# First transfers, scales and skip weights of a four-layer gated kernel in another order

## The chip, the cores and the metric

The kernel runs on one core of a Trainium2 chip. The core has five engines that work side by side and wait for each other through semaphores: TensorE (PE in the profile; PEld is its weight load), VectorE (DVE), ScalarE (ACT), GpSimd (POOL) and SyncE (SP), which here only issues transfers (DMAs). Every engine takes its own instructions in order. The metric is the time of one execution on the device in microseconds, as the median of several runs. A profile is one execution with every instruction recorded.

## The reference

The input `x` is 16 batches of 128 rows by 256 columns in float32, with a context of the same shape. Four layers follow each other; each adds a gated attention-like step and a gated feed-forward step to `x`:

```python
x = x + jnp.tanh(g_xattn[0]) * _L0_xattn_ref(ctx_2048, ctx_2048, _layernorm(x, axis=-1), L0_xattn_ssm_kernel, L0_xattn_D, 8)
x = x + jnp.tanh(g_ffn[0]) * _L0_ffn_ref(_layernorm(x, axis=-1), ...)
...
x = x + jnp.tanh(g_ffn[3]) * _L3_ffn_ref(_layernorm(x, axis=-1), L3_ffn_A, L3_ffn_B, L3_ffn_Wr, L3_ffn_br)
```

The change is in the first step. It forms the products of the context with itself within each head of 8 rows, convolves them along the 256 columns with the head's kernel, adds the products times a skip weight `D`, and weighs the result with the normalised `x`:

```python
kv = jnp.einsum('bhil,bhjl->bijhl', k_, v_)
...
y = jnp.fft.irfft(kv_f * kernel_f, n=fft_size)[..., :L]
out = y + kv * D[None, None, None, :, None]
out = jnp.einsum('bijhl,bhil->bjhl', out, q_)
```

The other steps are a mixture of experts, grouped attention, a quantised feed-forward layer, a retention, a second mixture of experts, a channel attention and a routed low-rank layer.

## The kernel before

**The start** (`stage_l0x`, line 461) is the first step. Its order of work on each engine is written out by hand (line 465). `x` comes in four groups of four batches, `xg[0]` to `xg[3]`; groups 0 and 1 are asked for on ACT's queue (lines 389 and 390), 2 and 3 on SP's (lines 590 and 591). The context comes transposed, in two halves of eight batches, by indirect gathers on POOL (`gathered`, line 363), two issues per half. The convolution is a matmul with a Toeplitz matrix per head: four transfers on SP (line 588) bring four heads each into `T[0]` to `T[3]`, a 128 by 256 block per head. The skip weight of a head is added on DVE to the antidiagonal of its block's first half, in place (line 608); `skips` holds the weights (line 393).

For each group `stats` (line 472) takes mean and variance on DVE, `scaled` (line 478) makes scale and offset with three operations on POOL, `normal` (line 488) applies them (on ACT; for group 1 on DVE, line 493), and `turn` (line 497) transposes the result on PE and copies it with ACT. Groups 2 and 3 get their sums from ACT (`scaled_by_act`) during the loop.

The loop (line 625) runs over 32 half heads: 16 heads for each of two halves of the batches. For each, `products` (line 520) multiplies context rows on POOL, in two operations (lines 527 and 528); `convolved` (line 531) runs 12 matmuls on PE; `weighed` (line 547) multiplies the result by the normalised `x` on DVE, in two operations (lines 551 and 552), and for some half heads POOL adds two halves of it (line 555); `summed` (line 557) reduces it on DVE. Iteration `n` weighs `n`, convolves `n + 2`, makes the products of `n + 4` and sums `n - 2`. Six buffers hold products, three hold convolutions. Before the loop come the first products and convolutions, and a loop over the 16 heads (lines 606 to 613) that adds all skip weights, with the normalisation of group 1 after the second and the reduction `some` of the mask after the tenth.

**The expert layer** (`stage_moe0`) follows from about 100 to 260 us, with its order by hand too. SP loads its weights during the start.

**The planned stage** (`stage_rest`, line 1183) is everything else, to the end. A list of operations goes to a planner (`Plan`, line 100), which picks at each step, per engine, among operations that are ready the one with the least target time plus biases: for a change of ACT's table, for a change of PE's mode, and for PE's idle time. The target of an operation is an entry of one of the `T_` tables plus an entry of `BASES` (lines 41 to 85); the biases are line 40:

```python
BIASES = 0.27, 158.38, 2.24, 0.00, 3.82
```

They are the window, the two biases for table and mode, the one for idle time, and a hold for wide results. Targets decide the order alone.

Of the kernel before, what the change touches and what calls it, by code (L numbers as in the profile page):

```python
# [11 lines left out]
F32 = mybir.dt.float32  # L12
# [3 lines left out]
ALU = mybir.AluOpType  # L16
AX = mybir.AxisListType
PSUM = bass.MemoryType.PSUM

P = 128  # L20
B = 16
# [15 lines left out]
NSH = 9  # L37
PAIR = 1
N_K1, N_K2, N_K4, N_R2, N_X = 10, 9, 5, 4, 7
BIASES = 0.27, 158.38, 2.24, 0.00, 3.82  # L40
T_ONCE = [
    -43.5, 143.5, 65.9, 105.9, -39.2, 199.6, -61.2, 86, 110.2, 143.6, 119.7, 115.6, 86.5, 65.9, 97.7, 4.3, -130.6,
    -31.9, -83.7, -176.3, -222, -116.8,
]
T_SHARED = [
    -108.2, -94.6, -22, -76.2, -45.3, -33.5, -4.1, -135.1, -8.9, 127.9, -47.6,
]
T_GROUPED = [
    -98.3, 41.7, 87, -96, -142.1, 41.2, 20, 103.7, -31.8, 38.5, 65.2, -33.5, 105.3, 116.7, -11.8, 15.6, 5.6, 10.4, 48,
    93.6, 22.1, -23.5, -1.1, 24.6, 24, 33.6, 88.5, 39, 44.3, 74.3, 49.7, 82.9, 62.6, 35, 15.8, 53.7, -88.1,  # L50
]
T_QUANTISED = [
    74.6, 108.2, 143.8, 35.5, -20.4, 108.8, 93.2, 70.8, 54.8, 0.9, 56.9, 75.7, 44.1, 78.4, 22.4, 76.5, 76.9, 78.3,
    68.4, 112.1, 95.9, 101.6, 168.9, 71.1, 70.5, 160.4, 125.7, 66.7, 86.5, 81.7, 88.9, 3.9,
]
T_RETENTION = [
    60.8, 125.2, 70.9, 96.4, 85.4, 184.2, 100.8, 158.9, 94.8, 114.2, 85.3, 76.2,
]
T_EXPERTS = [
    -18.4, 71.7, 93.4, 160.1, 16, 135.7, 102.6, 68.2, 141.5, 103.8, 168.9, 114.9, 137.7, 94.1, 66.8, 91.5, 63.4,  # L60
    117.2, 130.4, 135.6, 102.3, 81.9, 82.6, 136.4, 76.6, 117, 149.9, 147.8, 163.1, 49.5, 105.5, 66.3, 127.3, 116,
    63.5, 79.9, 129.9, 129.4, 243.9, 222, 155.6, 193.1, 140.4, 110.2, 84.4, 144, 133.2, 120.2, 112.1, 120.8, 152.2,
    151.4, 143.8, 119.1, 73.1, 148.2, 140.3, 171.3, 134.9, 139.5, 186.8, 147.2, 118.4, 105.7, 150.5, 149.6, 115.6,
    112.6, 101.4, 68.6,
]
T_CHANNEL = [
    106.3, 121.5, 94.5, 209.2, 127.9, 260.4, 293.5, 134.3, 140.5, 133.7, 128.7, 148.1, 303, 213.1, 146.4, 193, 142.3,
    140.6, 151.8, 126.6, 118, 194.7, 170.1, 152.9, 110.2, 143.9, 136.8, 170.3, 184.7, 172.7, 116.6, 100.5, 102.5,
    180.1, 162.7, 310.9, 187.6, 224.5, 189.8, 179.8, 191.8, 191.2, 236.3, 195.2, 230.7, 339.1, 313.4, 176.2, 162.1,
    179.1, 199.2, 177.8, 189.2, 185.4, 200.9, 265.5, 110.7, 187.9, 292.7, 192.9, 203.6, 214, 206.4, 264.8, 215.4,  # L70
    203.5, 198.3, 209.9, 204.3, 216.5, 310.7, 221.5, 193.6, 203.4, 223.9, 215.2, 227.3, 221.3, 275.4,
]
T_LOW_RANK = [
    397.4, 354.4, 300.9, 203.2, 200.5, 224.6, 225.4, 240.3, 233.7, 228.6, 226.9, 174.6, 163.2, 189.9, 262.2, 248.6,
    174.2, 209.8, 194.7, 253.1, 331.3, 215.7, 312.5, 243.8, 330.4, 253.6, 242.6, 202.8,
]
BASES = [
    -30.9, 31.3, -42.3, -30, -43.2, 35.7, 52.7, -91, -49.1, -4.9, -46.5, -16.6, -11.7, 30.9, -13.9, 41.5, 16.4, 23.3,
    8.9, 71.6, 56.7, 52.3, 67.2, 63, 63.8, 114.1, 95.4, 94.2, 108.9, 108.2, 48.7, 149.2, 150.6, 140.8, 143.9, 147.1,
    152.2, 191.7, 175.1, 210.6, 188.2, 190.8, 189.1, 232, 216.9, 224.2, 232.5, 229.3, 202.4, 271.9, 245.5, 273.5,  # L80
    268.1, 270, 274.8, 315.8, 317.8, 288.7, 312.9, 311.8, 316.5, 359.4, 348.6, 365.3, 355.4, 349.3, 358.2, 398.6,
    377.3, 409.5, 394.9, 392.3, 392.4, 438.6, 432.8, 421.6, 435.1, 433.5, 424.6, 465, 442.4, 462.7, 468.3, 468.4, 492,
    506.8, 485.5, 500.4, 493.9, 497.4, 575.3, 540.8, 525.4, 550.1, 524.4, 529.8, 628.8, 566, 560.1, 545.6, 558, 557.2,
    591,
]


# [257 lines left out]
def kernel(ctx: ExitStack, tc: tile.TileContext, a: dict, out: bass.AP):  # L345
    nc = tc.nc
# [9 lines left out]
    s0 = s0e.enter_context(tc.tile_pool(name="s0", bufs=1, side="right"))  # L356
# [6 lines left out]
    def gathered(u):  # L363
        for c in range(2):
            nc.gpsimd.indirect_dma_start(
                out=ctxT[:, u, c, :],
                out_offset=None,
                in_=a["ctxT"].rearrange("d (u b) s -> (d u) (b s)", u=2),
                in_offset=bass.IndirectOffsetOnAxis(ap=back[:, u, c : c + 1], axis=0),
            )  # L370
# [6 lines left out]
    anti = s0.tile([P, P], F32, name="anti")  # L377
# [8 lines left out]
    def asked(eng, g):  # L386
        eng.dma_start(xg[g], a["x"][g * GB : (g + 1) * GB].rearrange("b p d -> p b d"))

    asked(nc.scalar, 0)
    asked(nc.scalar, 1)  # L390
    T = [s0.tile([P, 4, D], F32, name=f"toep{q}") for q in range(4)]
    skips = s0.tile([P, B], F32, name="skips")
    nc.sync.dma_start(skips, a["L0_xattn_D"].partition_broadcast(P))
# [13 lines left out]

    tg = cst.tile([P, 8], F32, name="tg")
    for i, n in enumerate(("g_xattn", "g_ffn")):
        nc.gpsimd.dma_start(tg[:, 4 * i : 4 * i + 4], a[n].partition_broadcast(P))  # L410

    neghalf = cst.tile([P, GB], F32, name="neghalf")
    nc.gpsimd.memset(neghalf, -0.5)
# [47 lines left out]
    def stage_l0x(xTs, anyk, kba, rowsd, loads, xs, xnp, xns, rss, offs):  # L461

        with tc.tile_pool(name="s0w", bufs=2) as s0w, tc.tile_pool(name="s0t", bufs=2, space=PSUM) as pst, tc.tile_pool(
            name="s0y", bufs=3, space=PSUM
# [4 lines left out]
            mb = s0.tile([B, P], F32, name="mb")  # L469
            mvs, tmp = {}, {}  # L470

            def stats(g, of=range(GB)):
                if of[0] == 0:
                    mvs[g] = s0w.tile([P, GB, 2], F32, name="mv", bufs=4), s0w.tile([P, GB, 6], F32, name="st", bufs=4)
                mv, st = mvs[g]
                statistics([xg[g][:, k, :] for k in of], mv[:, of[0] :], st[:, of[0] :])

            def scaled(g):
                mv, _ = mvs[g]
                ve = s0w.tile([P, GB], F32, name="ve", bufs=4)  # L480
                scale_offset(mv, ve, rss[:, g], offs[:, g])
# [6 lines left out]
            def normal(g):  # L488
                tmp[g] = s0w.tile([P, GB, D], F32, name="xn")
                if g != 1:  # L490
                    return normalised(tmp[g], xg[g], rss[:, g], offs[:, g])
                for k in range(GB):
                    nc.vector.tensor_scalar(
                        tmp[g][:, k, :], xg[g][:, k, :], rss[:, g, k : k + 1], offs[:, g, k : k + 1], ALU.mult, ALU.add
                    )
# [94 lines left out]
            asked(nc.sync, 2)  # L590
            asked(nc.sync, 3)
            loads()
            gathered(1)
            warm = pst.tile([P, 512], F32, name="tp")
            for k in range(24):
                nc.tensor.transpose(warm[:, k % 4 * P : k % 4 * P + P], ident, ident)
            stats(0)
            scaled(0)
            nc.gpsimd.dma_start(rows[1:2, :], a["mask"].rearrange("(o b) s -> o (b s)", o=1))
            nc.gpsimd.dma_start(mb, a["mask"])  # L600
            stats(1)
            normal(0)
            products(0)
            scaled(1)
            turn(0)
            for n in range(B):
                t = T[n // 4][:, n % 4, 0:P]
                nc.vector.scalar_tensor_tensor(t, anti, skips[:, n : n + 1], t, ALU.mult, ALU.add)
                if n == 1:
                    normal(1)  # L610
                if n == 9:
                    some = s0.tile([B, 1], F32, name="some")
                    nc.vector.tensor_reduce(some, mb, AX.X, ALU.max)
            products(1)
            convolved(0)
            turn(1)
            products(2)
            convolved(1)
            products(3)
            scales = {}  # L620
            for g in (2, 3):
# [3 lines left out]
            for n in range(N):  # L625
                if n == N - 4:
                    turned(0)
                if n + 2 < N:
                    convolved(n + 2)
                if n in (18, 20, 22, 24):  # L630
                    back_turn(n - 18)
                weighed(n, n % 5 in (1, 3) or n >= 26)
                if n + 4 < N:
                    products(n + 4)
                if n > 1:
                    summed(n - 2)
                if n in (3, 5):
                    g = 2 + n // 5
                    scales.pop(g)()
                    normalised(tmp[g], xg[g], rss[:, g], offs[:, g])  # L640
                if n in (6, 10):
                    turn(2 + n // 10)
                if n == 9:
                    masks()
                if n in (18, 20, 22, 24):
                    added(n - 18)
                if n in (20, 24):
                    scales[n // 24] = scaled_by_act(n // 24, kept_tile(n // 24))
                if n in (22, 26):
                    scales.pop(n // 26)()  # L650
                    kept(n // 26)
# [1548 lines left out]
```

## Time and profile before

| what | value |
|---|---|
| median of 3 runs | 1080.39 us (1078.98 to 1081.77) |
| profiled execution | 1072.21 us, of it 1070.2 us between first and last instruction (the span) |
| PE, DVE, ACT, POOL busy | 91%, 69%, 57%, 50% of the span |
| granted TensorE clock, mean | 0.973 of full speed |
| start's loop, first weighing | 26.45 us |
| expert layer, about | 100 to 260 us |

A line of a timeline gives an instruction's start in us from the span's start, its duration, its engine, its line in the kernel, the operation, and what it writes and reads; a bracket at the end is the time that the engine stood idle before it and what ended that. Several equal instructions in a row are one line with a count. `toep` are the Toeplitz blocks, `kv` the products, `y` the convolutions, `pr` the weighed results, `xn` a normalised group, `tp` a transposed one, `st` and `mv` the statistics, `rss` and `offs` scale and offset.

### The profile page before, as it was taken

The page shows a single profiled execution, that of the slowest core. Times are in us where ns is not written, and L with a number is a line of the kernel's source. Part 1 is how long each engine was busy: PE and PEld are TensorE (multiplying, and loading weights), DVE is VectorE, ACT ScalarE, POOL GpSimd, SP SyncE. Part 2 cuts the span into 40 slices and gives each one's busy share as a digit, 9 for nine tenths or more (in the row PEclk, how much of TensorE's full clock was granted, in tenths as well). Part 3 has the DMA queues.
Part 4 walks back from the last instruction along what each step waited for, and adds up shares of the span by engine and source line. Part 5 has one row for each costly group of instructions (what it writes and reads, how often), then busy time and mean ns, then how long its engine had stood idle before and what let it go on. Part 6 is the DMA issues. An engine that isn't in the chain of part 4 may idle for free. (4 is left out here: it accounts for less than half of the span.)

```text
span 1070.2 us, 20227 instructions
## 1 busy us (share of the span) xinstructions
PE 978.4 (91%) x7076; PEld 715.2 (67%) x7076; DVE 736.9 (69%) x1763; ACT 612.0 (57%) x1066; POOL 538.3 (50%) x1027
## 2 busy tenths in 40 slices
PE   6998999998987898889999899899999999999987
PEld 5887777776665665756667576676766667567644
DVE  5998655524566587757687787787768778777643
ACT  3416422322255446767675867768777488676752
POOL 7899255421345653544465554755636462744311
PEclk8999999999998888999999999999999999999999
DMA  9712524344920033030321303313130303232220
GB/s 296 157 39 83 184 65 113 99 99 108 334 80 21 30 80 95 17 99 17 105 71 61 106 17 109 101 36 95 32 99 23 99 24 84 86 100 71 56 47 15
DMA packets 75152, 92.39 MB, mean 86 GB/s; under 512 B 10345, under 2 KB 65321, under 8 KB 75049
## 3 DMA queue, kind: packets, MB, share of 16 engines
q1 hardware_dynamic: 67276, 73.55, 24.2%
q0 software_dynamic: 6720, 16.51, 5.6%
q8 instruction: 57, 0.93, 0.4%
q10 hardware_dynamic: 1056, 1.05, 0.3%
q14 instruction: 43, 0.35, 0.1%
HBM read 57.51 MB, written 30.56 MB: 82 GB/s over the span
## 5 line engine op out<-in xcount | busy, mean ns | idle before, releaser
L1849 DVE TENSOR_REDUCE sg<-ps 128x4 f32<-128x1024 f32 x128 | 153.3, 1216 | 38.8 <-PE ps L1837 37.0
L1905 ACT ACTIVATE k<-ps 128x1024 f32<-128x1024 f32 x128 | 127.9, 1029 | 21.4 <-PE ps L1894 19.1
L1702 PE MATMUL ps<-L2w,r 128*128 128x512 f32 x384 | 101.4, 408 | 2.3 <-ACT k L1905 1.3
L1727 POOL TENSOR_TENSOR k<-k,sg 128x352 f32<-128x352 f32 (+4 forms) x112 | 56.2, 524 | 80.0 <-DVE k L1715 63.9
L1702 PEld LDWEIGHTS ps<-L2w,r 128*128 128x128 f32 x384 | 69.5, 189 | 21.5 <-ACT k L1905 3.2
L1327 POOL TENSOR_TENSOR sm<-sm,kconsts 128x1 f32<-128x1 f32 x96 | 19.9, 209 | 126.1 <-DVE sm L1326 119.8
L539 PE MATMUL y<-kv,toep 128*128 128x128 f32 (+1 forms) x384 | 70.0, 341 | 6.4 <-DVE pr L552 3.9
L1349 ACT COPY k<-pa 128x256 f32<-128x256 f32 (+1 forms) x79 | 35.0, 445 | 63.4 <-PE pa L1342 48.6
L539 PEld LDWEIGHTS y<-kv,toep 128*128 128x128 f32 x384 | 61.4, 198 | 14.4 <-issue 3.6
L1837 PE MATMUL ps<-gk,gq 64*128 64x256 f32 x512 | 57.9, 317 | 11.6 <-DMA gq<-dq 5.7
L1894 PE MATMUL ps<-gq,gk 64*128 64x256 f32 x512 | 60.0, 321 | 5.7 <-DVE nc L1454 1.6
L1837 PEld LDWEIGHTS ps<-gk,gq 64*128 64x128 f32 x512 | 38.4, 188 | 36.8 <-issue 16.4
L1342 PE MATMUL pa<-ident,k 128*128 128x128 f32 x268 | 51.0, 291 | 10.1 <-POOL k L1332 3.8
L933 POOL DMA_INDIRECT xb<-xs,who x40 | 39.4, 984 | 41.4 <-PE tb L945 33.2
L1894 PEld LDWEIGHTS ps<-gq,gk 64*128 64x128 f32 x512 | 38.6, 187 | 32.2 <-issue 10.7
L1328 POOL TENSOR_TENSOR sm<-sm,kconsts 128x1 f32<-128x1 f32 x96 | 55.3, 576 | 6.4
L1332 POOL TENSOR_SCALAR k<-x,sm 128x256 f32<-128x256 f32 x96 | 53.8, 561 | 7.5
L1325 DVE BATCH_NORM_STATS2 sm<-x 128x6 f32<-128x256 f32 x96 | 40.5, 422 | 21.1 <-POOL x L1954 11.9
L963 PE MATMUL ub<-L0we,xbT 128*128 x160 | 50.7, 460 | 0.2 <-ACT xbT L947 0.2
L1342 PEld LDWEIGHTS pa<-ident,k 128*128 128x128 f32 x268 | 31.1, 144 | 28.6 <-POOL k L1332 6.5
L1914 PE MATMUL pa<-k,v 128*32 128x256 f32 x768 | 49.1, 383 | 1.1 <-ACT k L1771 0.8
L1712 ACT ACTIVATE k<-ps 128x512 f32<-128x512 f32 x48 | 28.5, 597 | 32.9 <-PE ps L1702 26.7
(442 smaller groups left out, 2541.3 us busy)
## 6 DMA issues: line engine op xcount, KB each, us to landing
gq<-dq SPq DMA_DIRECT2D x64, 192.0 KB
dk<-r SPq DMA_DIRECT2D x32, 256.0 KB
gk<-dk SPq DMA_DIRECT2D x64, 128.0 KB
dq<-r SPq DMA_DIRECT2D x32, 256.0 KB
ys<-ysb SPq DMA_DIRECT2D x20, 256.0 KB
L0we<-in_L_w_dram SPq DMA_DIRECT2D x6, 704.0 KB
L2w<-in_L_w_dram POOLq DMA_DIRECT2D x3, 768.0 KB, 8.8
toep<-in_kpad_dram SPq DMA_DIRECT2D x4, 512.0 KB
```

The costliest lines, as they stand in the source:

```text
L539: nc.tensor.matmul(dst, lhsT=T[n % B // 4][:, n % 4, d : d + P], rhs=kv[k][:, H * mc : H * mc + H], start=(mc == 0 and k == 0), stop=(mc = ...
L963: nc.tensor.matmul(t[:, i, 0 : 2 * I], lhsT=xbT[:, i, c, :], rhs=we[:, bass.ds(regs[s][i] + c * 2 * I, 2 * I)], start=(c == 0), stop=(c == 1),
L1328: op("POOL", 0.53, lambda: G.tensor_tensor(s.t[:, 11:12], s.t[:, 10:11], nhalf, ALU.pow), r=[s], p=[s])
L1332: lambda: G.tensor_scalar(xn.t, x.t, s.t[:, 8:9], s.t[:, 11:12], ALU.add, ALU.mult),
L1342: lambda: [T.transpose(t.t[:, c * P : (c + 1) * P], xn.t[:, c * P : (c + 1) * P], ident) for c in range(n)],
L1702: T.matmul(u.t[:, 512 * k : 512 * k + 512], lhsT=xv()[:, m // 2, m % 2], rhs=wt[:, m // 2, c0 : c0 + 512], start=(m == 0), stop=(m == 3),)
L1727: G.tensor_tensor(v, v, bc(c(12)[:, e : e + k], 2, (hi_ - lo_) // k), ALU.mult)
L1837: T.matmul(mv[:, h, jj, :], lhsT=q.t[r, o + (t0 + n) * P : o + (t0 + n + 1) * P], rhs=k.t[r, o : o + D], start=True, stop=True,)
L1849: lambda m=m, nm=nm, ii=ii, tt=t0 + n: S.tensor_reduce(nm.t[:, 0:16].rearrange("p (t h j) -> p t h j", t=2, h=2)[:, tt, :, 2 * ii : 2 * ii ...
L1894: T.matmul(sv[:, h, jj, :], lhsT=k.t[r, o + (c0 + n) * P : o + (c0 + n + 1) * P], rhs=q.t[r, o : o + D], start=True, stop=True,)
L1905: op("ACT", 1.03, lambda s=s, pt=pt: A.activation(pt.t, s.t, AF.Exp), r=[s], w=[pt], tbl="exp")
L1914: T.matmul(av.t[g_ : g_ + 32, ii * D : (ii + 1) * D], lhsT=vt.t[:, sc, 8 * h + 4 * jh + 2 * ii + jj, :], rhs=pv[:, h, jj, :], start=(sc == 0),
```

## The change

The start is reordered; no operation is added or taken away there. Groups 0 and 1 of `x` and the two gate vectors are asked for on SP's queue. POOL makes the scales of groups 0 and 1 before the first products. The second gather and the two transfers of the mask come behind the third product. Skip weights of heads 0 to 3 are added before the normalisation of group 1 and those of heads 4 to 7 behind it; those of heads 8 to 15 go into the first four iterations of the loop, two in each, and `some` into the fifth. The transpose of group 1 goes ahead of the first convolution on PE. The planned stage gets new target times and biases; its operations stay.

```diff
-BIASES = 0.27, 158.38, 2.24, 0.00, 3.82
+BIASES = 0.27, 154.01, 2.49, 0.00, 3.84
 T_ONCE = [
-    -43.5, 143.5, 65.9, 105.9, -39.2, 199.6, -61.2, 86, 110.2, 143.6, 119.7, 115.6, 86.5, 65.9, 97.7, 4.3, -130.6,
+    -59.8, 128.2, 45.3, 90.8, -64.4, 173.4, -76.7, 71.1, 104.3, 141.6, 130.2, 109.8, 88.5, 89.8, 114.2, 17.6, -141.3,
...
-    asked(nc.scalar, 0)
-    asked(nc.scalar, 1)
+    asked(nc.sync, 0)
+    asked(nc.sync, 1)
...
     for i, n in enumerate(("g_xattn", "g_ffn")):
-        nc.gpsimd.dma_start(tg[:, 4 * i : 4 * i + 4], a[n].partition_broadcast(P))
+        nc.sync.dma_start(tg[:, 4 * i : 4 * i + 4], a[n].partition_broadcast(P))
...
             loads()
-            gathered(1)
             warm = pst.tile([P, 512], F32, name="tp")
             for k in range(24):
                 nc.tensor.transpose(warm[:, k % 4 * P : k % 4 * P + P], ident, ident)
+
+            def with_skip(n):
+                t = T[n // 4][:, n % 4, 0:P]
+                nc.vector.scalar_tensor_tensor(t, anti, skips[:, n : n + 1], t, ALU.mult, ALU.add)
+
             stats(0)
             scaled(0)
+            stats(1)
+            scaled(1)
+            normal(0)
+            products(0)
+            turn(0)
+            for n in range(4):
+                with_skip(n)
+            normal(1)
+            products(1)
+            turn(1)
+            convolved(0)
+            for n in range(4, 8):
+                with_skip(n)
+            products(2)
+            convolved(1)
+            gathered(1)
             nc.gpsimd.dma_start(rows[1:2, :], a["mask"].rearrange("(o b) s -> o (b s)", o=1))
             nc.gpsimd.dma_start(mb, a["mask"])
-            stats(1)
-            normal(0)
-            products(0)
-            scaled(1)
-            turn(0)
-            for n in range(B):
-                t = T[n // 4][:, n % 4, 0:P]
-                nc.vector.scalar_tensor_tensor(t, anti, skips[:, n : n + 1], t, ALU.mult, ALU.add)
-                if n == 1:
-                    normal(1)
-                if n == 9:
-                    some = s0.tile([B, 1], F32, name="some")
-                    nc.vector.tensor_reduce(some, mb, AX.X, ALU.max)
-            products(1)
-            convolved(0)
-            turn(1)
-            products(2)
-            convolved(1)
             products(3)
...
                 weighed(n, n % 5 in (1, 3) or n >= 26)
+                if n < 4:
+                    with_skip(8 + 2 * n)
+                    with_skip(9 + 2 * n)
+                if n == 4:
+                    some = s0.tile([B, 1], F32, name="some")
+                    nc.vector.tensor_reduce(some, mb, AX.X, ALU.max)
                 if n + 4 < N:
```

All the other tables (`T_SHARED` to `T_LOW_RANK` and `BASES`) get new numbers in the same way, most of them within some 20 of the old ones.

## The prediction

> **What bounds the kernel now.** I read the page first, then the windows (busy time by stretch), then the timelines of the first 40 us, engine by engine.
>
> The engine shares, from the page:
> ```profile
> PE 978.4 (91%) x7076; PEld 715.2 (67%) x7076; DVE 736.9 (69%) x1763; ACT 612.0 (57%) x1066; POOL 538.3 (50%) x1027
> ```
> TensorE (PE) is the busiest, but not everywhere. The windows (length, then PE, PEld, DVE, ACT, POOL busy, PE clock, DMA share, GB/s):
> ```profile
> 27.00:60.00 33.00, 31.60 (x184) 28.63 (x185) 30.83 (x44) 12.58 (x34) 30.51 (x38) 0.95 0.65 142
> 60.00:75.00 15.00, 14.83 (x94) 13.57 (x93) 14.45 (x22) 1.42 (x7) 13.58 (x17) 1.00 0.11 33
> 75.00:100.00 25.00, 22.23 (x130) 18.73 (x129) 24.37 (x36) 12.17 (x39) 23.46 (x28) 1.00 0.13 43
> ...
> 340.00:440.00 100.00, 87.88 (x621) 65.07 (x619) 71.37 (x177) 52.17 (x87) 54.58 (x113) 0.87 0.21 57
> ...
> 700.00:850.00 150.00, 142.48 (x1216) 100.67 (x1217) 113.96 (x288) 106.69 (x170) 81.88 (x172) 1.00 0.24 67
> ```
> From 27 to 100 us, the loop over 32 half heads, VectorE (DVE) is busy 69.65 of 73 us, with GpSimd (POOL) close behind (67.55). Work on DVE is the limit there: DVE idle time removed before the loop is a gain, DVE work only moved is not. In the planned stage, from 260 us on, PE is the limit, but at 340 to 440 us it is busy 88% at a clock of 0.87, later 95% at 1.00.
>
> DVE's timeline of the start (start, duration, then what; idle time before it in brackets):
> ```profile
> 14.91 0.88 DVE L608 SCALAR_TENSOR_TENSOR toep<-anti,skips,toep 128x128 f32<-128x128 f32 x2
> 17.00 3.38 DVE L493 TENSOR_SCALAR xn<-x,rss,offs__125 128x256 f32<-128x256 f32 x4 [1.21 <-POOL offs__125 L433]
> 20.31 4.46 DVE L608 SCALAR_TENSOR_TENSOR toep<-anti,skips,toep 128x128 f32<-128x128 f32 x8
> 24.69 0.27 DVE L613 TENSOR_REDUCE some<-mb 16x1 f32<-16x128 f32 x1
> 24.88 1.64 DVE L608 SCALAR_TENSOR_TENSOR toep<-anti,skips,toep 128x128 f32<-128x128 f32 x6
> 26.45 0.67 DVE L551 TENSOR_TENSOR pr<-y,qT 128x512 f32<-128x512 f32 x1
> ```
> DVE waits for x until 7.98, then 1.85 and 1.21 us: 11.04 us idle before the first weighing (26.45). Three of the skip additions singly, and the POOL operations beside the first two:
> ```profile
> 20.31 1.12 DVE L608 SCALAR_TENSOR_TENSOR toep<-anti,skips,toep 128x128 f32<-128x128 f32 x1
> 21.36 0.70 DVE L608 SCALAR_TENSOR_TENSOR toep<-anti,skips,toep 128x128 f32<-128x128 f32 x1
> 24.43 0.34 DVE L608 SCALAR_TENSOR_TENSOR toep<-anti,skips,toep 128x128 f32<-128x128 f32 x1
> ```
> ```profile
> 20.20 1.08 POOL L527 TENSOR_TENSOR kv<-ctxT 128x512 f32<-128x512 f32 x1
> 21.25 0.66 POOL L528 TENSOR_TENSOR kv<-ctxT 128x256 f32<-128x256 f32 x1
> ```
> The reader is to see the lock step: beside a product on POOL the same addition lasts as long as the product, 1.12 or 0.70 us; after 23.57, when POOL stands still, 0.34, a new one each 0.26. The four normalisations of line 493 show the same (3.38 us against 1.38 for four of them at 111 us with POOL idle).
>
> **The change, part by part.** As marker I take the start of the fifth weighing, 33.74 us now: by then all moved additions are done in both kernels.
>
> *Transfers.* Moved on SP ahead of the skip weights, the constants and the four Toeplitz transfers: two x transfers (1.02 us of issue on ACT) and two gate vectors (0.62 and 0.59 on POOL). By 15 us 4.06 MB have moved: 2.05 on the gathers' queue, 1.05 of x, 0.96 on SP's. x lands earliest when 1.05 MB go alone at the 370 GB/s seen from 5 us on, about 6.3 us; latest as now, 7.98 and 12.26. I take 6.3 and 8.5. Everything behind them on SP (Toeplitz, x 2 and 3, weights) is issued some 2 us later. x 2 and 3 now end ACT's wait at 22.71 and feed POOL's scales at 36.29; the expert weights wait until 97: covered, and without cover each us late costs one.
>
> *Gather.* The second gather (two issues, 2.33 us with their gap) and the mask's two DMAs (1.16 us) go behind the third product on POOL. Their readers come late (products of the second half near 53 us; the reduction of the mask, now fifth in the loop). Without the second gather's 1 MB the first lands earlier: the first product, 13.73 now, starts between 12.0 and 13.73; I take 12.5, since half of the 2.05 MB on that queue goes away but x and Toeplitz remain.
>
> *Scales first.* POOL makes both scales (1.6 us each) before the products: mean 8.75, scale 10.3; second 11.2, then 12.9, or 0.4 us after the gather. Three products take 3 x (1.04 + 0.62) = 5.0 us: 12.9 to 17.9.
>
> *Four additions, then four normalisations.* Toeplitz 0 lands in 11.5 to 14 us (first addition 14.91 now); I take 12.6. One addition passes freely, six operations fall in lock step with the six products, the last is free (0.35): the second normalisation ends at 18.2, in place of 20.31. Its transposes end 0.9 us later (20.31 to 21.22 now): 19.1. Additions 4 to 7 cost nothing: they pass under the transposes and the first convolution, at 0.26 while POOL issues DMAs; in lock step they would end at 21.5, still before the weighing below.
>
> *First convolution after the second transpose.* On PE it now took 3.67 us at a granted clock of 0.50 (15.63 to 19.30); two took 4.09 at 1.00, 2.05 each. Bounds 2.05 and 3.67; PE is a little busy before, so I take the middle, 2.9: the first weighing starts at 22.0 less a trifle, 21.9, bounds 20.5 to 22.9, in place of 26.45.
>
> *Eight additions in the loop.* From first to fifth weighing 7.29 us pass now. After the change two additions follow each of four weighings, and the mask's reduction (0.27) precedes the fifth. POOL is in products or pair sums (1.28 us) nearly without pause, so I go through it: of the eight, two come when POOL waits for a weighing (0.26 each), six wait for an operation of 1.04, 0.62 or 1.28, mean 0.83 by the pair above: 0.5 + 5.0 + 0.27 = 5.8, less the 0.51 us that DVE waits for PE before the fifth weighing now. The marker lands at 21.9 + 7.29 + 5.3 = 34.5: 0.75 late. DVE waits another 0.51 us at 38.14, and POOL leads by some 2 us then, so most is absorbed. Start: 0, bounds -4.2 (20.5, all eight at 0.26 and no wait: 29.5) and +4 (22.9, all eight behind a sum of 1.28).
>
> [...]
>
> [...]
>
> *Expert layer, 100 to 260 us.* Same instructions, shifted by the start.
>
> *Planned stage.* 810 us; new target times and slightly other biases: same operations and durations, another order. PE is busy 739.8 of it. Bounds: 290 to 440 us has a PE share of 0.866, 560 to 1000 one of 0.947; if a new order lifts the first to the second, 150 x 0.081 = 12 us go; if it drops another 150 us to the first's share, 12 come. The trace favours neither; I take 0, as the operations are the same.
>
> Sum: 0 + 0. The profiled execution took 1072.21 us (span 1070.2 and 2.0 around it), so 1072.2 again; the median of three runs stands 8.2 above it, so 1080.4 in those terms.
>
> **The rivals.** About 0.3%, 3.2 us, is what a measurement of this kernel can tell from no change.
>
> 1. The planned stage gains: the weak 290 to 440 us fill up. For it: PE at 0.866 there and 0.87 clock, so there is room. Against: nothing in the trace says that new targets use it. Two thirds of 12 us: 1072. Chance 0.24.
> 2. The start gains: the additions find POOL waiting, since it runs out of work behind the weighings (now 5.43 us at 23.57). Price up to -4.2: 1076. Chance 0.14. Against: POOL has two DMAs and a product to catch up.
> 3. Slower, by the additions in the loop alone: each of eight waits behind a pair sum, 8 x (1.28 - 0.26) = 8.2 us over free additions, 3.2 over my sum, with the first weighing late besides. It decides from the point where the first weighing plus 12.6 us exceeds 33.74 + 0.5 + 3.2 = 37.4, that is a first weighing after 24.8 us, or additions that cost over 1.2 us each. About 1085. Chance 0.10.
> 4. The planned stage loses as much as it could gain: 1088. Chance 0.19.
> 5. The transfers don't come sooner, as the sum of bytes sets the time: x at 7.98 and 12.26. Then the second scale is ready at 16.8, the first weighing at about 23, start +1: still no measurable change, and part of my forecast's chance.
>
> **How the numbers follow.** Forecast (start near 0, planned stage within 3 us): 0.33, 1080.4 us. Faster is 1 and 2, 0.38; slower 3 and 4, 0.29; within 0.3% the rest, 0.33. Forecast's own range 1077 to 1084. The whole range adds the start's bounds to three quarters of the planned stage's (9 us), 1069 to 1090; it leaves out 2 in 10 or fewer.
>
> **What would show it.** First statistics near 6.3 us, second directly behind; second scale before the first product; the second normalisation's end near 18.2; first weighing at 20.5 to 22.9; the loop's additions at 0.7 to 1.3 us each, not 0.34; fifth weighing near 34.5; loop's end within 2 us of now. In the windows, 100 to 260 us of the same length; the PE share of 290 to 440 us tells rivals 1 and 4. I am wrong if the first weighing comes before 19 us with free additions, or if the planned stage's length moves by over 3 us: its order is what I could not read from the profile.

## The result, and the profile after

The changed kernel took 1087.76 us (median of 11 runs, 1080.47 to 1091.11), the kernel before 1080.79 us (11 runs): ratio over all runs 1.0053, 95% interval 1.0035 to 1.0071 (the medians alone lie 0.64% apart). It is slower, by more than the 0.3% that I had called no change. Two later comparisons gave 1.0012 (0.9987 to 1.0037) and 1.0033 (1.0005 to 1.0062). The profiled execution took 1086.43 us, with a span of 1084.4 us.

First the engine shares of the changed kernel, from its page:

```profile
PE 974.1 (90%) x7076; PEld 709.7 (65%) x7076; DVE 739.9 (68%) x1763; ACT 611.6 (56%) x1066; POOL 538.3 (50%) x1025
```

The work is the same: 739.9 us on DVE against 736.9, less on PE. No engine is busy for more than 3 us longer, so most of the 14 us by which the span is longer are waiting, not work. The windows of the changed kernel (length, then PE, PEld, DVE, ACT, POOL busy, PE clock, DMA share, GB/s):

```profile
27.00:60.00 33.00, 30.49 (x185) 27.32 (x184) 31.74 (x45) 10.10 (x23) 29.68 (x37) 1.00 0.64 137
60.00:75.00 15.00, 14.44 (x87) 12.57 (x86) 14.52 (x21) 0.91 (x4) 13.83 (x17) 1.00 0.15 46
75.00:100.00 25.00, 22.20 (x131) 19.05 (x130) 24.37 (x36) 12.27 (x40) 22.84 (x29) 1.00 0.13 43
...
340.00:440.00 100.00, 80.17 (x624) 56.05 (x621) 73.05 (x193) 57.85 (x98) 58.73 (x117) 0.97 0.23 61
...
700.00:850.00 150.00, 142.79 (x1164) 100.93 (x1165) 113.59 (x308) 112.58 (x179) 81.83 (x173) 0.99 0.25 74
```

DVE is still the limit from 27 to 100 us: 70.63 of 73 us, 69.65 before. Where it lost is seen in its timeline of the start (below it, the fifth weighing and the loop's last reduction of the kernel before):

```profile
4.88 0.43 DVE L426 BATCH_NORM_STATS2 st<-x 128x6 f32<-128x256 f32 x1 [4.88 <-DMA x<-in_x_dram]
...
13.24 3.20 DVE L599 SCALAR_TENSOR_TENSOR toep<-anti,skips,toep 128x128 f32<-128x128 f32 x4 [3.42 <-DMA toep<-in_kpad_dram]
16.36 1.90 DVE L493 TENSOR_SCALAR xn<-x,rss,offs__125 128x256 f32<-128x256 f32 x4
18.18 2.02 DVE L599 SCALAR_TENSOR_TENSOR toep<-anti,skips,toep 128x128 f32<-128x128 f32 x4
23.59 0.69 DVE L551 TENSOR_TENSOR pr<-y,qT 128x512 f32<-128x512 f32 x1 [3.38 <-PE y L539]
...
24.80 0.61 DVE L599 SCALAR_TENSOR_TENSOR toep<-anti,skips,toep 128x128 f32<-128x128 f32 x2
...
26.82 1.63 DVE L599 SCALAR_TENSOR_TENSOR toep<-anti,skips,toep 128x128 f32<-128x128 f32 x2
...
29.57 1.54 DVE L599 SCALAR_TENSOR_TENSOR toep<-anti,skips,toep 128x128 f32<-128x128 f32 x2
...
33.55 1.62 DVE L599 SCALAR_TENSOR_TENSOR toep<-anti,skips,toep 128x128 f32<-128x128 f32 x2
...
35.88 0.69 DVE L551 TENSOR_TENSOR pr<-y,qT 128x512 f32<-128x512 f32 x1
...
102.00 0.69 DVE L558 TENSOR_REDUCE xT<-pr 128x128 f32<-128x512 f32 x1 [0.27 <-POOL pr L555]
```
```profile
33.74 0.69 DVE L551 TENSOR_TENSOR pr<-y,qT 128x512 f32<-128x512 f32 x1 [0.51 <-PE y L539]
...
100.34 0.69 DVE L558 TENSOR_REDUCE xT<-pr 128x128 f32<-128x512 f32 x1 [0.27 <-POOL pr L555]
```

The first statistics start 3.1 us sooner (4.88, not 7.98) and the first weighing 2.86 us sooner (23.59, not 26.45). But the fifth starts 2.14 us later (35.88, not 33.74): the eight additions in the loop took 5.4 us on DVE (0.61 + 1.63 + 1.54 + 1.62), in place of 2.1 at 0.26 each. Five of the eight lasted 0.34 to 0.50 us; three met a pair sum or a product on POOL and lasted 1.12 to 1.37. The loop's last reduction ends at 102.69 us, before at 101.02. DVE still waits 3.42 us for the first Toeplitz block and 3.38 us for the first convolution, whose cause PE's timeline and the window of its slow stretch show:

```profile
17.21 2.44 PE L502 MATMUL tp<-ident,xn 128*128 128x128 f32 x8 [5.47 <-DVE xn L493]
19.44 4.83 PE L539 MATMUL y<-kv,toep 128*128 128x256 f32 x16
```
```profile
13.40:23.60 10.20, 6.33 (x21) 5.26 (x22) 6.82 (x13) 4.44 (x17) 9.72 (x13) 0.50 1.12 341
```

From 13.4 to 23.6 us PE was granted half its clock; it had stood idle 5.47 us before the second group's transposes.

### The profile page after: what moved, and what is told of

It reads as the page before. It is cut to its first block, busy times and chain, and to the rows that moved or that the text cites. A ratio compares the mean times of both kernels' runs of the same rounds, so it can differ in the third digit from the quotient of the medians.

```text
span 1084.4 us, 20213 instructions
## 1 busy us (share of the span) xinstructions
PE 974.1 (90%) x7076; PEld 709.7 (65%) x7076; DVE 739.9 (68%) x1763; ACT 611.6 (56%) x1066; POOL 538.3 (50%) x1025
## 4 chain that ended last, share of the span: by engine, by line
PE 49%; DVE 19%; ACT 12%; DMA 6%; issue 6%; POOL 5%; SPq 2%; another core or an unknown queue 1%; ACTq 0%; DVEq 0%; POOLq 0%
PE ps L1710 6%; PE ub L971 4%; DVE sg L1857 4%; ACT k L1913 3%; PE yb L997 3%; PE ps L1845 3%; PE pa L1922 2%; DVE xT L558 2%; DMA gq<-dq 2%; PE pa L2004 2%; PE pa L1350 2%; PE up L737 2%; PE pa L1759 2%; DVE pr L551 2%; PE ps L1902 2%
## 5 line engine op out<-in xcount | busy, mean ns | idle before, releaser
L1710 PEld LDWEIGHTS ps<-L2w,r 128*128 128x128 f32 x384 | 69.2, 188 | 20.5 <-ACT k L1913 2.2
```

What stands on the lines that cost most here:

```text
L1710: T.matmul(u.t[:, 512 * k : 512 * k + 512], lhsT=xv()[:, m // 2, m % 2], rhs=wt[:, m // 2, c0 : c0 + 512], start=(m == 0), stop=(m == 3),)
```

## The experiments

All are compared with the kernel before on their own chip. The table has the times of the start (us; first profile of each) and the ratio. Over the twelve rows that have a ratio, a loop that ends 1 us later goes with 1.04 us more time (correlation 0.84).

| kernel | first weighing | fifth | loop's last reduction ends | ratio (95% interval) |
|---|---|---|---|---|
| before, first profile | 26.45 | 33.74 | 101.02 | |
| before, second profile (e3) | 25.07 | 31.95 | 99.66 | |
| new tables alone (e2) | 25.26 | 32.14 | 99.87 | 0.9988 (0.9969 to 1.0007) |
| changed | 23.59 | 35.88 | 102.69 | 1.0053 (1.0035 to 1.0071) |
| changed again (e5) | 22.82 | 34.97 | 101.76 | 1.0012 (0.9987 to 1.0037) |
| changed again (e11) | 22.49 | 34.64 | 101.47 | 1.0033 (1.0005 to 1.0062) |
| new start alone (e1) | 23.02 | 35.16 | 101.98 | 1.0020 (1.0001 to 1.0039) |
| e1, additions ahead of the loop (e4) | 25.81 | 32.70 | 100.44 | 1.0003 (0.9983 to 1.0024) |
| e1, PE kept busy (e7) | 22.70 | 34.85 | 101.64 | 0.9998 (0.9975 to 1.0021) |
| e1, normalisation first (e6) | 18.32 | 35.40 | 102.18 | 1.0029 (1.0008 to 1.0050) |
| changed, normalisation first (e8) | 18.18 | 35.28 | 102.08 | 1.0022 (1.0000 to 1.0044) |
| e6, additions ahead of the loop (e9) | 23.94 | 31.54 | 98.61 | 0.9992 (0.9967 to 1.0016) |
| e6 without the loop's additions (e10) | 17.84 | 27.87 | 95.87 | 0.9972 (0.9947 to 0.9997) |
| e9, two additions partly on POOL (e12) | 24.76 | 32.07 | 99.34 | 0.9998 (0.9961 to 1.0036) |

**The two halves of the change.** e1 is the changed kernel with the tables of before, e2 the kernel before with the new tables. e3 is the kernel before, for a second profile.

```diff
 # e1, against the changed kernel (and all T_ tables and BASES as before)
-BIASES = 0.27, 154.01, 2.49, 0.00, 3.84
+BIASES = 0.27, 158.38, 2.24, 0.00, 3.82
 # e2, against the kernel before (and all T_ tables and BASES new)
-BIASES = 0.27, 158.38, 2.24, 0.00, 3.82
+BIASES = 0.27, 154.01, 2.49, 0.00, 3.84
```

> The changed start with the target times and biases of before. Theory A (two separate costs: the new start is later by what the profile of the change shows at the end of its loop, 102.7 against 101.0 us; the rest comes from the new order of the planned stage): ratio to before 1.0016 (+1.7 us), within 1.000 to 1.003, the loop's last reduction ending near 102.7 us. Rival B (the planned order is harmless; the start's shift sets transfers and clock windows against the later stages): ratio 1.005 as for the whole change. Rival C (the start is a gain and only the new targets cost): below 0.999.

> The start of before with the new target times and biases. Theory A: ratio 1.004 (+4 us), within 1.002 to 1.006; in the trace the planned stage takes 4 to 5 us longer from the end of the expert layer to the end. Rival B: 1.000. Rival C: 1.006 or more.

> The kernel before, unchanged, profiled a second time. In the profile of the change ACT and PE stand still for 6.5 us at 163 us, with no work of the program named as the cause, and the profile of before lacks it. If that stall is an event of single executions of either kernel, this second profile may have it or not, and its span lies at 1070 us without it or at 1077 to 1080 us with it; if it comes from the change, the span is 1070 us again and no such stall stands in the expert layer.

The start alone is slower (1.0020, about 2.2 us), though its interval only just clears 1; the tables alone are not told from no change. So the 4 us that theory A expected from the new order are not there, and the two parts don't add up to 1.0053. e3 shows two things. First, the start of before is not fixed: its fifth weighing came at 31.95 us here and at 33.74 in the profile that I predicted from; e2, whose start is that of before, has 32.14. Against this second profile the new start (the changed kernel and e1) ends its loop 2 to 3 us late in every profile (101.47 to 102.69, against 99.66), and e1's 2.2 us are of that size. Second, its span is 1079.7 us, 9.5 above the first profile. Comparing equal instructions, 6.9 us of that come at 140 to 160 us, in the expert layer, and 6.5 between 260 and 320. Most of the first is one wait of ACT, after which the next matmuls run slower (the eight of line 963 took 2.63 us ahead of it and 4.54 behind it; in the changed kernel, line 971, 2.63 and 3.97, with 0.50 of the clock granted from 167.0 to 173.8 us); in the timelines of before, of before again, and of the changed kernel:

```profile
161.33 0.46 ACT L971 ACTIVATE silb<-ub 128x352 f32<-128x352 f32 x1 [2.23 <-PE ub L963]
```
```profile
162.83 0.46 ACT L971 ACTIVATE silb<-ub 128x352 f32<-128x352 f32 x1 [5.13 <-remote]
```
```profile
168.97 0.46 ACT L979 ACTIVATE silb<-ub 128x352 f32<-128x352 f32 x1 [6.51 <-remote]
```

The first profile of before lacked a wait that the second has and the changed kernel has too; of the fourteen profiles it is the only one without it. So the jump of 7.8 us that the two first profiles show there, a large part of their 14 us, is not the change. What released that wait the trace does not say, and it stays open.

**The additions out of the loop.** e4 is e1 with the additions of heads 8 to 15 behind those of 4 to 7, ahead of the first weighing.

```diff
-            for n in range(4, 8):
+            for n in range(4, B):
                 with_skip(n)
...
-                if n < 4:
-                    with_skip(8 + 2 * n)
-                    with_skip(9 + 2 * n)
```

> As e1_start, but the skip additions of heads 8 to 15 stand right behind those of heads 4 to 7, ahead of the first weighing, where DVE waits 3.4 us for the first convolution in the profile of the change. Theory A, with additions in the loop locked to GpSimd's products at about 0.7 us each (eight took 5.4 us in the loop): the first weighing starts at about 24.5 us in place of 23.6, the loop is shorter by 5.4 us, so the loop ends some 4.5 us sooner than in e1_start, near 98.2 us; ratio to before 0.997. Rival D (additions in the loop cost nothing because DVE has slack there): no difference to e1_start.

First to fifth weighing then took 6.89 us, as in before (6.88 in e3), against 12.14 in e1; the loop ended 1.54 us sooner than in e1. The first weighing was 2.8 us later than e1's, though, so the expected end at 98.2 us and ratio of 0.997 did not come: one addition, at 20.50 us, lasted 3.20 us. The next experiments tell what held it.

**The changed kernel again, and the normalisation first.** e5 and e11 are the changed kernel. e6 and e8 put the second normalisation ahead of the first four additions, e6 in e1, e8 in the changed kernel. e7 gives PE 24 transposes without use between the two groups' transposes.

```diff
 # e6 and e8
+            normal(1)
             for n in range(4):
                 with_skip(n)
-            normal(1)
 # e7
             turn(0)
+            more = psy.tile([P, B, 8, 8], F32, name="y").rearrange("p b i j -> p (b i j)")
+            for k in range(24):
+                nc.tensor.transpose(more[:, k % 8 * P : k % 8 * P + P], ident, ident)
```

> The changed kernel again, beside the others on one chip, because the parts so far (start alone 1.002, targets alone 0.999) don't add up to the 1.0053 of the whole. Theory E (the parts add up within their intervals; the planned stage is as long as before and the start's 2 to 3 us are all there is): ratio 1.002 to 1.004, loop's end near 102.5 us, and a planned stage within 1.5 us of the others. Rival F (the new targets cost more behind the new start than behind the old one): 1.005 again.

> As e1_start (changed start, targets of before), with the second normalisation moved ahead of the four additions that wait for the Toeplitz transfer. In e1_start DVE stands still from 9.8 to 13.7 us for that transfer while the scales of the second group are ready at 11.1. Theory G (the place of that wait sets the first weighing): the normalisation ends near 13 in place of 18.9 us, the first convolution starts near 14.5, the first weighing comes at 17.5 to 19 in place of 23.0, the loop ends at 97 to 98.5 in place of 102.0 us, the ratio to before is 0.997 to 0.999. Rival H (GpSimd and its locked additions set it): the first weighing at 21 us or later, the loop's end within 1 us of 102.

> As e6_norm_first, but with the new target times and biases. Theory E: as fast as e6_norm_first within 0.2%. Rival F: slower than e6_norm_first by 0.3% or more.

e5's ratio, 1.0012, lies under what both of its theories said, with the loop's end at 101.76. e8 is as fast as e6 (1.0022 and 1.0029), so the new tables cost nothing there. In e6 the first weighing did come at 18.32 us, 4.7 sooner than in e1; the four normalisations took 1.38 us, with POOL idle. But the fifth weighing came at 35.40, no sooner than e1's. DVE's timeline of e6, and POOL's beside it:

```profile
18.32 0.67 DVE L551 TENSOR_TENSOR pr<-y,qT 128x512 f32<-128x512 f32 x1
...
22.02 6.28 DVE L599 SCALAR_TENSOR_TENSOR toep<-anti,skips,toep 128x128 f32<-128x128 f32 x1
```
```profile
21.16 1.09 POOL L527 TENSOR_TENSOR kv<-ctxT 128x512 f32<-128x512 f32 x1
22.16 0.66 POOL L528 TENSOR_TENSOR kv<-ctxT 128x256 f32<-128x256 f32 x1
22.73 1.08 POOL L527 TENSOR_TENSOR kv<-ctxT 128x512 f32<-128x512 f32 x1
23.73 0.65 POOL L528 TENSOR_TENSOR kv<-ctxT 128x256 f32<-128x256 f32 x1
24.30 1.30 POOL L555 TENSOR_TENSOR pr<-pr 128x512 f32<-128x512 f32 x1
25.53 1.06 POOL L527 TENSOR_TENSOR kv<-ctxT 128x512 f32<-128x512 f32 x1
26.53 0.62 POOL L528 TENSOR_TENSOR kv<-ctxT 128x256 f32<-128x256 f32 x1
27.10 1.05 POOL L527 TENSOR_TENSOR kv<-ctxT 128x512 f32<-128x512 f32 x1
28.09 0.68 POOL L528 TENSOR_TENSOR kv<-ctxT 128x256 f32<-128x256 f32 x1
```

One addition that takes 0.34 us elsewhere lasted 6.28 us, as long as POOL's operations followed each other without a pause: it outlasted eight of them in a row and ended 0.21 us into the ninth, the last. POOL then stood idle for 4.47 us, until a weighing on DVE gave it work: its run ended where its next operation needed DVE. In e8 the same addition lasted 6.30 us. What was won ahead of it was lost in it.

> As e1_start, with 24 more idle transposes on PE between the transposes of group 0 and those of group 1, where PE stands still for 6 us and its clock is then granted at half. Theory I (half clock on the first convolutions makes the first weighing late): the first convolution takes 2.1 in place of about 3 us, the first weighing starts at 21.5 in place of 23.0, the loop ends 1 to 1.5 us sooner, ratio 1.001. Rival J (the weighing is late for other reasons): first weighing unchanged within 0.5 us.

e7's PE timeline:

```profile
11.61 2.78 PE L614 MATMUL y<-ident 128*128 128x128 f32 x24
17.32 2.44 PE L502 MATMUL tp<-ident,xn 128*128 128x128 f32 x8 [2.92 <-DVE xn L493]
```

The window of its slow stretch (columns as above):

```profile
18.00:21.40 3.40, 3.30 (x12) 2.73 (x13) 2.31 (x5) 2.19 (x8) 3.10 (x5) 0.50 1.15 324
```

The 24 transposes shortened PE's idle time from 5.47 to 2.92 us, yet the second group's eight transposes took the same 2.44 us, and the first weighing came at 22.70, against 22.82 in e5 on the same chip. Keeping PE busy so far ahead does not bring it sooner. That does not refute theory I, though: the half clock came later (in e5 it lasted from 14.74 to 21.57 us), but it ended at the same point, so the first convolution, from 19.55 us, still began at half clock. That e7's ratio lies below e1's has no cause in the start that I can show.

**What the additions cost.** e9 is e6 with the loop's additions ahead of the first weighing, as in e4; e10 is e6 without them, so it leaves out the skip weights of heads 8 to 15.

```diff
 # e9, against e6
-            for n in range(4, 8):
+            for n in range(4, B):
                 with_skip(n)
 # e9 and e10, against e6
-                if n < 4:
-                    with_skip(8 + 2 * n)
-                    with_skip(9 + 2 * n)
```

> This is the kernel with the second normalisation first (the changed start, old tables), with the additions of heads 8 to 15 taken out of the loop and put behind those of heads 4 to 7, ahead of the first weighing. In the kernel with the normalisation first one addition in the loop (at 22.02 us) lasted 6.28 us, through seven POOL operations that followed each other without a pause; that took back all of the 4.7 us by which its first weighing was sooner. Theory J (it is only the additions beside POOL's products that took the gain): here they pass between 18.3 and 21.2 us, while POOL issues transfers, at 0.26 each but one of 1.1; first weighing 21.0 to 21.5, fifth 27 to 28.5, the loop's last reduction at 95 to 96.5, in place of 99.66 in the second profile of before and of 102 with the normalisation first. Time 0.9955 to 0.9985 of before. Rival K (GpSimd or TensorE takes over as the limit as soon as DVE is early): first weighing as said, loop's end at 98 or later, time 0.999 to 1.001. A third case: the last addition meets the product that POOL starts at 21.2 and is held as long as the one at 22.02 was: fifth weighing 33 or later, time 1.000 to 1.003.

> The kernel with the second normalisation first, with the additions of heads 8 to 15 left out altogether: the skip weights of these heads are missing from what it computes. It shows what the start could be worth if they cost nothing. Theory J: first weighing 18.3, fourth near 25 (its product is made behind the transfers that POOL issues), fifth near 27, loop's last reduction at 94.5 to 96, some 6 us before that of the kernel with the additions in the loop; time 0.994 to 0.998 of before. Rival K: the loop's end not before 98, time 0.999 to 1.001, that is, the loop additions cost nothing that the other engines would not have taken.

> The changed kernel once more, since its first comparison gave 1.0053 and its second 1.0012. Theory E (the loop ends 2 us later than with the kernel before in its own second profile and nothing else differs): 1.001 to 1.003. If the first comparison stands: 1.004 to 1.007.

e11's ratio, 1.0033, lies between its two theories. With no additions in the loop (e10) the loop ended at 95.87, 6.3 us before e6, and the kernel is faster: 0.9972 (0.9947 to 0.9997). GpSimd and TensorE take back a part (the fourth weighing waits 2.86 us for its convolution), but not all, as rival K had it. In e9, which computes everything, the last addition was held, as in the third case, but for half as long as that case said: the fifth weighing came at 31.54, not after 33. The loop's end and the ratio lie where rival K put them, for this other reason. DVE's timeline, and POOL's beside it:

```profile
20.84 3.19 DVE L599 SCALAR_TENSOR_TENSOR toep<-anti,skips,toep 128x128 f32<-128x128 f32 x1
23.94 0.68 DVE L551 TENSOR_TENSOR pr<-y,qT 128x512 f32<-128x512 f32 x1
```
```profile
20.68 0.55 POOL L620 DMA_DIRECT2D mb<-in_mask_dram  x1
21.21 1.09 POOL L527 TENSOR_TENSOR kv<-ctxT 128x512 f32<-128x512 f32 x1
22.21 0.66 POOL L528 TENSOR_TENSOR kv<-ctxT 128x256 f32<-128x256 f32 x1
22.78 1.08 POOL L527 TENSOR_TENSOR kv<-ctxT 128x512 f32<-128x512 f32 x1
23.78 0.71 POOL L528 TENSOR_TENSOR kv<-ctxT 128x256 f32<-128x256 f32 x1
```

While POOL issues transfers the additions pass at 0.26 each, but one of 1.15; the last of all begins during a transfer's issue, meets the products and is held 3.19 us, while the weighings beside POOL's products, with one input from PSUM, stay at 0.68. The loop ended at 98.61, sooner than in any profile of before, but by too little to be told in the time.

e12 takes two additions off that row: DVE multiplies their antidiagonals by the weights early, and POOL adds both at once behind its fourth product.

```diff
+            scaled_anti = s0.tile([P, 2, P], F32, name="scan")
+            for n in range(2):
+                nc.vector.tensor_scalar(scaled_anti[:, n, :], anti, skips[:, B - 2 + n : B - 1 + n], None, ALU.mult)
             for n in range(4):
                 with_skip(n)
...
-            for n in range(4, B):
+            for n in range(4, B - 2):
                 with_skip(n)
...
             products(3)
+            last = T[B // 4 - 1][:, 2:4, 0:P]
+            nc.gpsimd.tensor_tensor(last, last, scaled_anti, ALU.add)
```

> The kernel with the normalisation first and all additions ahead of the first weighing, in which the last addition (of head 15, at 20.84 us) was held for 3.19 us by the products that POOL starts at 21.2. Here heads 14 and 15 leave DVE's row of additions: DVE makes skip weight times antidiagonal for these two while it waits for the first Toeplitz transfer (12.65 to 13.5 us), and POOL adds both to their blocks in one operation behind its fourth product. Theory J (a DVE operation with two SBUF inputs that meets POOL's unbroken run is held to the run's end, and only that was left): the row of additions ends at 20.3 to 20.9, first weighing 20.3 to 21.2 in place of 23.94, fifth 28 to 29.5 in place of 31.54, the loop's last reduction 96 to 97 in place of 98.61; the weighings, with one input from PSUM, stay at 0.67 to 0.69 us beside POOL. Time 0.9955 to 0.9985 of before. Rival: the last of the remaining additions is held all the same, first weighing 23.5 or later, or POOL's extra operation sets the products back: loop's end 98 or later, time 0.998 to 1.002.

My expectation failed: the rival's side came. The two multiplications ran beside the first products (13.68 to 15.30) in place of idle time and pushed the first addition back from 13.50 to 15.22; the thirteenth began at 20.35, not at 19.24 as in e9, and was held for 3.87 us:

```profile
20.35 3.87 DVE L599 SCALAR_TENSOR_TENSOR toep<-anti,skips,toep 128x128 f32<-128x128 f32 x1
```

So the hold itself is shown again, at another addition, but that a free row would make the whole kernel measurably faster than before is not: of what computes everything, no version beat before.

## Where the prediction was right, and where it was wrong

The measured time, 1087.76 us, lies in the range of 1069 to 1090. The forecast of no change within 0.3% did not hold in the first comparison (0.53%); the two later ones (0.12% and 0.33%) lie within it and at its edge, and the first of these is not told from no change. That the range held says little of the start: added up as the prediction says, its terms give 1067 to 1093, and 9 us on either side of that are the planned stage's. By steps:

- *Transfers*: direction right, size off. x landed at 4.88 us, below my earliest 6.3, and the second group was there when the first statistics ended (7.22). The rate held (368 and 380 GB/s from 3 to 5 us); 6.3 charged the first group with the bytes of both, 1.05 MB, where it needs half of them.
- *Gather*: first product 11.98 us, for 12.5; at the edge of its bounds (12.18 and 12.25 in the later profiles).
- *Scales first*: right in order, 1.9 us sooner than said (second scale 11.04, for 12.9); POOL then waited 0.94 us for the gather, so nothing came of it.
- *Four additions, then four normalisations*: 18.26 us for 18.2. Two errors cancelled: the Toeplitz block came at 13.24, not 12.6, and fewer operations fell in lock step, since the products were sooner.
- *First convolution after the second transpose*: mis-sized. I took the middle between both clocks, 2.9 us; from the end of the transposes (19.65) to the first weighing 3.94 passed, above my upper bound of 3.67, and the transposes themselves ended 0.55 late. Both ran at half clock (0.50 granted). The bound was low: the convolution that it was read from ran only in part at half clock (from 15.60 to 19.30 us the granted clock was 0.59 on average, not 0.50). First weighing 23.59, for 21.9, outside its bounds of 20.5 to 22.9; 22.82 and 22.49 in the later profiles, within them.
- *Eight additions in the loop*: right in the sum, 12.29 us from first to fifth weighing, for 12.6, but not in its make-up: five passed nearly freely, not two, three lasted longer than the mean of 0.83, and the mask's reduction came behind the fifth weighing, not ahead of it.
- "*Most is absorbed*": this step failed. From the fifth weighing to the loop's end 67.28 us passed before and 66.81 after: 0.47 of 2.14 us absorbed. In all other kernels of the table it is 66.8 to 68.0. DVE's waits of over 0.15 us in this stretch were 0.95 us in all before and 0.27 after: 0.68 us was all the reserve that could be used, and the mask's reduction took 0.2 of it. Being late at the fifth weighing is nearly all being late at the end.
- *Start: 0*. It was 1.7 us late against the first profile of before and 2 to 3 against the second, within my bounds of -4.2 and +4. (The upper one comes out only with some 2.5 us absorbed: 22.9 + 7.29 + 8 x 1.28 + 0.27 - 0.51 is 40.2, 6.5 late.) Besides the clock and the absorption it lacked a better baseline: the marker of before, 33.74, lies at 31.95 in its second profile, where the second x transfer was there 2.7 us sooner (statistics at 9.55, not 12.26). e2, with the same start, has them at 9.72. The idle time that the change was to remove was partly not there in two other executions.
- *Expert layer*: the same, shifted, but for the wait on line 979 (971 in before), which before has as well in its second profile.
- *Planned stage*: 0 was not contradicted. From 260 us to the end the shift against the first profile of before grew by 4.7, 9.5 and 0.4 us in the three profiles of the changed kernel, and by 5.6 in before's own second profile, so the 3 us that I named as a sign of being wrong say nothing. Over all profiles it grew by 5.8 us on average with the new tables (five, 0.4 to 9.5) and by 4.4 with the old ones (eight, -1.0 to 5.8). The tables alone took 0.9988. Rivals 1 and 4, at 8 us and more, are not what the tables alone show; a difference of some 2 us is not excluded. The window of 340 to 440 us (PE busy 80.17 against 87.88 us) does not tell, since it holds other work after a shift of 15 us.
- *Rivals*: rival 3 had the mechanism, additions in the loop, and nearly the time (1085), though neither of its conditions held: the first weighing did not come after 24.8, and the additions cost 0.68 us on average, not over 1.2. Its price was mis-sized as well: 8 x 1.28 is 4.7 us over my sum's 5.5, not 3.2. Rival 5 fell with x at 4.88, rival 2 since three of the additions found POOL at work.

What stays open is the rest of the first comparison: 1.0053 is 5.7 us, of which the start explains 2 to 3. The second (1.3 us) and the third (3.6 us) need no rest, or next to none. Within one kernel the time goes with the mean granted clock of a run: over the 35 runs of before beside e5 by 7.9 us per 0.01 (correlation -0.83). The first comparison's runs of the changed kernel had a median clock of 0.970, the second's 0.976. That fits, but the runs of before beside the first have no clock on record, so it is not shown.

## What to carry to other kernels

Before moving an operation on DVE like these additions, look at what POOL does in the new place: beside POOL's transfers most passed at 0.26 us (e9), while beside an unbroken run of POOL's operations one of 0.34 us was held for up to 6.30 (e8). Here, work that was moved within the engine that is the limit reappeared at the end nearly one for one: 2.14 us at the fifth weighing, 1.67 at the loop's end. Take a second profile of the kernel before where single microseconds decide: here its fifth weighing came at 33.74 and at 31.95 us, and its span was 1070.2 and 1079.7 us.

## What was not expected of the hardware

- A DVE operation of 0.34 us was held for 3.19, 3.20, 3.87, 6.28 and 6.30 us (e9, e4, e12, e6, e8), each time to 0.21 to 0.24 us after the start of the last POOL operation of an unbroken run. Elsewhere, beside the first products and in the loop, one DVE operation passed with each POOL operation (1.12 and 0.70 us). One thing tells the two apart in the traces: all five holds lie in a run that follows POOL's transfer issues without a wait; every DVE operation that passed with one product or sum, while more of the run was to come, did so in a run that POOL began after waiting. Whether that is the cause is open; no run tests it.
- The half clock outlasted the idle time: in the changed kernel PE worked from 17.21 us on and had the full clock only at 23.6, 6.4 us later; in e5 it was 4.2 us, in e11 3.3. In the starts of the fourteen profiles PE is granted half clock in stretches of 3.41, 6.83 or 10.24 us (before 6.83 and 3.41, the changed kernel 10.24), one, two or three times the same length. What ends such a stretch is not shown.
- A wait in the expert layer of 3.7 to 6.5 us on ACT whose release the trace does not show; of the fourteen profiles only the first of before lacks it.
